# A graph network on one core: the recurrent layer's first state turned to features by VectorE squares and a DRAM trip

## The chip, the cores and the metric

The kernel runs on one core of a Trainium2 chip. The core has five engines with queues of their own: TensorE (PE, with its weight loads PEld) multiplies matrices into PSUM, VectorE (DVE) and ScalarE (ACT) work elementwise, GpSimd (POOL) does small things here, and SyncE (SP) issues DMAs. The metric is the device time of one execution in microseconds; lower is better. All arithmetic is in float32.

## The reference

A batch of 32 graphs with 512 nodes and 128 features per node passes four layers, each `x = x + layer(relu(layernorm(x)))`. All share one adjacency matrix. Cut to what is computed:

```python
# x: (32, 512, 128), adj: (512, 512)
# layer 0: graph convolution
x = x + einsum(A_norm, h) @ W.T + b            # A_norm: normalized adj + I
# layer 1: gated recurrent layer, five steps; h starts as relu(layernorm(x))
def step(h):
    m  = einsum('nm,bmd->bnd', adj, h)         # both of its matrices are adj
    av = concatenate([m, m], -1)
    u3 = h @ u3_w.T + u3_b
    z  = sigmoid(av @ w3_w.T + w3_b + u3)
    r  = sigmoid(av @ w4_w.T + w4_b + u3)
    hv = tanh(av @ w5_w.T + w5_b + (r * h @ u5_w.T + u5_b))
    return (1 - z) * h + z * hv
x = x + step(step(step(step(step(h)))))
# layers 2 and 3: graph attention (leaky relu, masked softmax over neighbours)
x = x + elu(softmax(mask(leaky(e_src + e_dst))) @ (h @ W))
x = x + softmax(mask(leaky(e_src + e_dst))) @ (h @ w)
```

The step needs its state `h` in two layouts. The product with `adj` sums over nodes, so it wants nodes on the partitions. The gates sum over features, so they want features on the partitions.

## The kernel before

The program is drawn up as a list of operations with an engine, a cost, a due time, and the tiles read and written. A greedy list scheduler simulates the engines with these costs and fixes, before the program is built, in which order each engine gets its instructions and which buffer each value uses. Every engine then runs its own list in order. Two batches make a pair; products with `adj` are done for a pair together with seven block products in place of eight.

The buffers that matter below (cut):

```python
    plan = Plan({
        "bank": tiles(8, TOKENS, "bank", psum),
        "lane": list(range(LANES)),
        "x": tiles(13, TOKENS, "x"),
        "h": tiles(LANES, [P, 2, 2 * D], "h"),
        "sq": tiles(2, [P, Q, W * C], "sq"),
        "far": tiles(4, [Q, W, Q, W * C], "far", dram),
        "hT": tiles(LANES + 2, TOKENS, "hT"),
# ... cut
}, 174, 0.08)
```

`h` is the state with nodes on the partitions, `hT` the state with features on them. `sq` and `far` serve trips through DRAM. `LANES = 6` bounds the batches that are in the recurrent layer at one time.

The recurrent layer's start, for each batch of a pair. `norm_relu` writes `h`; `to_features` makes `hT` from it with four TensorE transposes into a PSUM bank, and ScalarE copies the bank to SBUF:

```python
    def ggnn(pair, due):
        hs, hTs, lanes = [], [], []
        for b in pair:
            lane, h, hT = Val("lane"), Val("h", 2), Val("hT")
            op("SP", 0.0, due - 3, lambda: None, r=[xs[b]], w=[lane], delay=0)
            op("SP", 0.0, due - 3, lambda: None, r=[lane], w=[h], delay=0)
            norm_relu(b, h, due - 3)
            p = to_features(h, due - 2, hT)
            op("ACT", A, due - 2, lambda p=p, hT=hT: nc.scalar.copy(flat(hT.t), flat(p.t)), r=[p], w=[hT])
            hs.append(h)
            hTs.append(hT)
            lanes.append(lane)
        for s in range(STEPS):
            now = due + LANES * s
            ms = products(*hs, of_adj, now)
            for i, b in enumerate(pair):
                hs[i], hTs[i] = step(b, s, ms[i], hTs[i], now + i, lanes[i])
```

```python
    def to_features(y, due, *then):

        p = Val("bank")

        def turns():
            for c in range(C):
                nc.tensor.transpose(p.t[:, c, :], chunk(y, c), ident.t)
        op("PE", C * TURN, due, turns, r=[y, ident], w=[p, *then])
        return p
```

The step reads `hT` first in the second matmul of its gate (`reset`), after the products `m`. Its new state is in feature layout; the way back to `h` for the next product is `shuttle`:

```python
    def step(b, s, m, hT, due, lane):
        gate, r, rh, z = Val("bank"), Val("r"), Val("rh"), Val("z")

        def reset():
            nc.tensor.matmul(flat(gate.t), gates.t[:, 0, :], flat(m.t), start=True, stop=False)
            nc.tensor.matmul(flat(gate.t), gates.t[:, 1, :], flat(hT.t), start=False, stop=True)
        op("PE", 2 * MM, due + 0.2, reset, r=[m, hT, gates], w=[gate])
        op("ACT", A, due, lambda: nc.scalar.activation(flat(r.t), flat(gate.t), AF.Tanh, bias=gate_b["w4"].t, scale=0.5),
           r=[gate, gate_b["w4"]], w=[r])
        op("DVE", V, due - 5, lambda: nc.vector.scalar_tensor_tensor(flat(rh.t), flat(r.t), 1.0, flat(hT.t), op0=ALU.add, op1=ALU.mult),
           r=[r, hT], w=[rh])
        op("PE", MM, due + 0.3, lambda: nc.tensor.matmul(flat(gate.t), gates.t[:, 2, :], flat(m.t), start=False, stop=True,
                                                   skip_group_check=True), r=[m, gates], w=[gate])
# ... cut: update gate, candidate, and the new state "new"
        if not last:
            shuttle(new, None, h, True, due, due - 5)
            return h, new
```

`shuttle` is the trip that the kernel already has. VectorE transposes 32x32 blocks into `sq`; four DMAs write it to DRAM, and two (or one) read it back so that the blocks land on the partitions where they belong:

```python
    def shuttle(src, squares, dst, halves, due, soon):


        sq, far = Val("sq"), Val("far", Q)
        if halves:
            for a in range(2):
                op("DVE", 0.34, soon, lambda a=a: nc.vector.transpose(
                    sq.t.rearrange("p q (a j l) -> p a q l j", a=2, l=2)[:, a],
                    flat(src.t).rearrange("p (a l q i) -> p a q l i", a=2, l=2, q=Q)[:, a]), r=[src], w=[sq])
        else:
            op("DVE", 0.61, soon, lambda: nc.vector.transpose(
                sq.t.rearrange("p q (c j) -> p q c j", c=C), flat(src.t).rearrange(squares, c=C, q=Q)), r=[src], w=[sq])
        for k in range(Q):
            op("SP", 0.44, due, lambda k=k: nc.sync.dma_start(
                far.t[:, :, k, :].rearrange("q i f -> i q f"), sq.t[k * W:(k + 1) * W]), r=[sq], w=[far[k]], delay=4)
        if halves:
            for a in range(2):
                op("SP", 0.4, due, lambda a=a: nc.sync.dma_start(
                    dst.t[:, a, :].rearrange("p (k f) -> p k f", k=Q),
                    far.t.rearrange("q i k (a f) -> a (q i) k f", a=2)[a]), r=[far], w=[dst[a]], delay=5)
        else:
            op("SP", 0.4, due, lambda: nc.sync.dma_start(
                dst.t if dst.kind != "h" else dst.t.rearrange("p a (k f) -> p (a k) f", k=2), far.t.rearrange("q i k f -> (q i) k f")),
               r=[far], w=[dst], delay=5)
```

It runs after all steps but the fifth, for the fifth step's result, and for the input of the attention layers; the last pairs take TensorE transposes instead, because then nothing is left to hide a trip behind.

Of the kernel before, what the change touches and what calls it, by code (L numbers as in the profile page):

```python
# [18 lines left out]
W = 32  # L19
Q = P // W  # L20
NEAR = 4
EASE = 0
LANES = 6


# [17 lines left out]
class Plan:  # L43
# [8 lines left out]
    def op(self, engine, cost, due, emit, r=(), w=(), delay=None):  # L52
        o = Op(engine, cost, due, emit, self.DELAY[engine] if delay is None else delay)
        o.id = len(self.ops)
        before = {}
        for items, writes in ((r, False), (w, True)):
            for item in items:
                v, parts = item if isinstance(item, tuple) else (item, None)
                parts = range(len(v.writers)) if parts is None else [parts]
                if v not in o.vals:  # L60
                    o.vals.append(v)
                    v.uses += 1
                for c in parts:
                    before.update((p.id, p) for p in v.writers[c])
                    if writes:
                        before.update((p.id, p) for p in v.readers[c])
        for items, writes in ((r, False), (w, True)):
            for item in items:
                v, parts = item if isinstance(item, tuple) else (item, None)
                for c in range(len(v.writers)) if parts is None else [parts]:  # L70
                    if writes:
                        v.writers[c], v.readers[c] = [o], []
                    else:
                        v.readers[c].append(o)
        before.pop(o.id, None)
        for p in before.values():
            p.then.append(o)
        o.waits = len(before)
        self.ops.append(o)
# [72 lines left out]
def gnn_stack(ctx: ExitStack, tc: tile.TileContext, a: dict, out: bass.AP):  # L152
    nc = tc.nc
    x, adj = a["x"], a["adj"]
    B, N, D = x.shape
    C = N // P
# [9 lines left out]
    def flat(t):  # L166
        return t.rearrange("p c k -> p (c k)")
# [3 lines left out]
# [5 lines that stand above are left out]
# [26 lines left out]
    op = plan.op  # L202
    MM, MM1, TURN = 0.858, 0.224, 0.111
    V, A = 0.61, 0.585
# [27 lines left out]
    for c in range(C):  # L232
        e, q = (("SP", nc.sync), ("ACT", nc.scalar))[c % 2]
        op(e, 0.45, -1001, lambda c=c, q=q: q.dma_start(adj_sb.t[:, c, :], adj[c * P:(c + 1) * P, :]),
           w=[adj_sb[c]], delay=3.6)
    xs = []
    for b in range(B):
        v = Val("x", C)
        op("SP", 0.95, max(-995 + b, STEPS * b - 20) if b >= 8 else -995 + b, lambda v=v, b=b: nc.sync.dma_start(v.t, x[b].rearrange("(c p) d -> p c d", p=P)),
           w=[v], delay=3)  # L240
# [23 lines left out]
    for c in range(C):  # L264
        p = Val("bank")

        def turn_adj(c=c, p=p):
# [5 lines left out]
           r=[adj_sb[c]], w=[deg[c]])  # L273
# [17 lines left out]
    for m in range(C):  # L291
        op("DVE", 0.7, -797, lambda m=m: nc.vector.scalar_tensor_tensor(
            anT.t[:, m, :], adjT.t[:, m, :], dinv.t[:, m:m + 1], flat(drow.t), op0=ALU.mult, op1=ALU.mult),
           r=[adjT, dinv, drow], w=[anT[m]])
        op("DVE", 0.26, -797, lambda m=m: nc.vector.scalar_tensor_tensor(
            block(anT.t, m), ident.t, dinv2.t[:, m:m + 1], block(anT.t, m), op0=ALU.mult, op1=ALU.add),
           r=[ident, dinv2], w=[anT[m]])
# [19 lines left out]
    for l in (2, 3):  # L317
        far = Val(None, C)
# [12 lines left out]
        for c in range(C):  # L331
            op("SP", 0.4, 4 + l, lambda l=l, c=c, far=far: nc.sync.dma_start(
                maskT[l].t[c * W:(c + 1) * W], far.t[:, :, c, :].rearrange("q i n -> i q n")),
               r=[far], w=[maskT[l][c]], delay=2.2)
# [33 lines left out]
    for k, u, half in (("w4", "u3", True), ("w3", "u3", True), ("w5", "u5", False)):  # L368
        gate_b[k] = fixed([P, 1], "gate_b" + k)
        op("DVE", 0.1, -14, lambda k=k, u=u: nc.vector.tensor_add(gate_b[k].t, raw["b" + k].t, raw["b" + u].t),  # L370
           r=[raw["b" + k], raw["b" + u]], w=[gate_b[k]])
# [4 lines left out]
    for i, l in enumerate((2, 3)):  # L376
        p = Val("bank")
        op("PE", 0.3, -9, lambda i=i, l=l, p=p: nc.tensor.matmul(p.t[:, 0, :2], gats.t[:, i, :], a_pair[l].t, start=True, stop=True),
           r=[gats, a_pair[l]], w=[p])
# [46 lines left out]
# [11 lines that stand above are left out]
# [19 lines left out]
        else:  # L456
            op("SP", 0.4, due, lambda: nc.sync.dma_start(
                dst.t if dst.kind != "h" else dst.t.rearrange("p a (k f) -> p (a k) f", k=2), far.t.rearrange("q i k f -> (q i) k f")),
               r=[far], w=[dst], delay=5)

    def products(h1, h2, factors, due):

        x1, x2, S = (h1[0], h1[1]), (h2[0], h2[1]), Val("S", 4)
        HV, HM, HA = 0.34, 2 * 0.432, 0.26

        def part(item):
            v, a = item
            return v.t[:, a, :]  # L470

        def combine(o, u, v, f):
            op("DVE", HV, due - 5, lambda: f(part(o), part(u), part(v)), r=[u, v], w=[o])  # L473
        add, sub = nc.vector.tensor_add, nc.vector.tensor_sub
        combine(S[2], x1[0], x2[0], sub)
        combine(S[0], x2[0], x2[1], add)
        combine(S[1], S[0], x1[0], sub)
        combine(S[3], x1[1], S[1], sub)
        m1, m2, p1, u2, u4, r, t = Val("m", 2), Val("m", 2), Val("half"), Val("half"), Val("half"), Val("bank"), Val("bank")

        def times(r, item, k, fresh, *also):
            def two():
                u = part(item).rearrange("p (f l) -> p l f", l=2)
                for l in range(2):
                    nc.tensor.matmul(low(r), u[:, l, :], factors[k][0]()[:, l, :], start=fresh and l == 0, stop=l == 1,  # L485
                                     skip_group_check=not fresh)
            op("PE", HM, due, two, r=[item, factors[k][1]], w=[r, *also])

        def copy(o, r, out):
            op("ACT", HA, due, lambda: nc.scalar.copy(out(), low(r)), r=[r], w=[o])  # L490

        def low(v):
            return flat(v.t)[:, :2 * P]

        def high(v):
            return flat(v.t)[:, 2 * P:]
        def add_up(o, u, out):
            op("DVE", HV, due - 5, lambda: nc.vector.tensor_add(out(), u.t, low(t)), r=[u, t], w=[o])  # L498

        times(r, x1[0], 0, True, m1, m2, t, p1, u2, u4)  # L500
        copy(p1, r, lambda: p1.t)
        times(t, x1[1], 3, True)
        add_up(m1[0], p1, lambda: low(m1))
        times(r, S[1], 1, False)
        copy(u2, r, lambda: u2.t)
        times(t, S[2], 4, True)
        times(r, S[0], 2, False)
        copy(u4, r, lambda: u4.t)
        add_up(m2[1], u4, lambda: high(m2))
        times(t, x2[1], 6, False)  # L510
        add_up(m2[0], u2, lambda: low(m2))
        times(r, S[3], 5, False)
        copy(m1[1], r, lambda: high(m1))
        return m1, m2
# [32 lines left out]
    def ggnn(pair, due):  # L547
        hs, hTs, lanes = [], [], []
        for b in pair:
            lane, h, hT = Val("lane"), Val("h", 2), Val("hT")  # L550
            op("SP", 0.0, due - 3, lambda: None, r=[xs[b]], w=[lane], delay=0)
            op("SP", 0.0, due - 3, lambda: None, r=[lane], w=[h], delay=0)
            norm_relu(b, h, due - 3)
            p = to_features(h, due - 2, hT)
            op("ACT", A, due - 2, lambda p=p, hT=hT: nc.scalar.copy(flat(hT.t), flat(p.t)), r=[p], w=[hT])
            hs.append(h)
            hTs.append(hT)
            lanes.append(lane)
# [7 lines that stand above are left out]
# [29 lines left out]
        h = None if last else Val("h", 2)  # L595
        if due >= STEPS * B - EASE:
            p = to_features(new, due + 2, *([] if last else [h]))
# [164 lines left out]
```

## Time and profile before

The kernel takes 1664.14 us (median of three runs, 1663.68 to 1665.16). The profiled execution has a span of 1661.8 us.

| engine | busy us | share of the span | instructions |
|---|---|---|---|
| TensorE matmuls (PE) | 1634.7 | 98% | 7422 |
| TensorE weight loads (PEld) | 1176.3 | 71% | 7422 |
| VectorE (DVE) | 1362.7 | 82% | 3836 |
| ScalarE (ACT) | 734.8 | 44% | 1657 |
| GpSimd (POOL) | 143.2 | 9% | 136 |
| DMA, mean of 16 engines | | 34% | 311,423 packets |

How to read it: busy time is the time in which at least one instruction of the engine ran. TensorE's instructions overlap, so their listed durations add up to more than its busy time. A float32 matmul appears as two instructions, a transpose as one. In the chain of waits the profiler goes back from the last instruction, each time to what released it, and so names the engines that set the end. "A <- B" in the list of waits says that A's engine stood idle before A until B was done. "SPq" is SyncE's queue, which issues the DMAs.

The TensorE transposes of the first state are those that write `bank` from `ident` and `h` (128 instructions, for 32 batches); ScalarE's copies of them write `hT` from `bank` (32).

### The profile page before, as it was taken

Reading aid. Unit: us, or ns where it says so; the run is one execution under the profiler, and the core shown is the slowest. Engines: PE = TensorE matmul, PEld = TensorE weight load, DVE = VectorE, ACT = ScalarE, POOL = GpSimd, SP = SyncE. Lnnn points to the kernel's source line nnn. Section 1 sums busy time; section 2 is a strip of 40 time slices with the busy share of each in tenths; the row PEclk is TensorE's granted clock in tenths of the full one; section 3 lists DMA queues with packets and bytes.
Section 4 is the critical chain, followed back from the end, with each engine's and each line's share of the span. In section 5 each row is a group of like instructions: output and inputs, shape, how many; then the busy total and the mean of one; then the engine's idle time right before and its main releaser. Section 6 shows DMA issues by size and latency. Waiting matters only on the chain.

```text
span 1661.8 us, 23750 instructions
## 1 busy us (share of the span) xinstructions
PE 1634.7 (98%) x7422; PEld 1176.3 (71%) x7422; DVE 1362.7 (82%) x3836; ACT 734.8 (44%) x1657; POOL 143.2 (9%) x136
## 2 busy tenths in 40 slices
PE   7999999999999999999999999999999999999998
PEld 5766667677776777777677776777777777766677
DVE  8966778888878888888788888888888878777888
ACT  4643453535345354433534335353443534333433
POOL 2200000001001110000100000000000000000100
PEclk9999999999999999999999999999999999999999
DMA  5222333433334343342423334333242423434100
GB/s 153 51 70 58 83 83 95 115 80 99 90 89 108 84 105 87 91 113 73 122 71 99 98 92 108 90 96 95 77 121 64 108 70 91 106 90 114 27 26 27
DMA packets 311423, 146.17 MB, mean 88 GB/s; under 512 B 150400, under 2 KB 292864, under 8 KB 311296
## 3 DMA queue, kind: packets, MB, share of 16 engines
q1 hardware_dynamic: 311008, 144.12, 34.4%
q8 instruction: 59, 0.97, 0.2%
q14 instruction: 68, 0.56, 0.1%
q10 hardware_dynamic: 288, 0.52, 0.1%
HBM read 80.48 MB, written 64.08 MB: 87 GB/s over the span
## 4 chain that ended last, share of the span: by engine, by line
PE 92%; DVE 5%; ACT 1%; issue 1%; DMA 0%; POOL 0%; SPq 0%; DVEq 0%; POOLq 0%; ACTq 0%
PE bank L485 33%; PE bank L699 12%; PE bank L570 8%; PE bank L569 8%; PE bank L576 8%; PE bank L583 8%; PE bank L584 8%; PE bank L644 3%; PE bank L541 2%; PE bank L688 1%; PE bank L432 1%; DVE st L390 1%; PE bank L520 0%; ACT y L407 0%; POOL rstd L397 0%
## 5 line engine op out<-in xcount | busy, mean ns | idle before, releaser
L485 PE MATMUL bank<-made,S 128*128 128x256 f32 x1140 | 276.3, 380 | 3.9 <-DVE S L473 1.8
L397 POOL TENSOR_TENSOR rstd<-ve,mhalf 128x4 f32<-128x4 f32 x128 | 141.4, 1107 | 1491.0 <-DVE ve L395 1193.6
L485 PEld LDWEIGHTS bank<-made,S 128*128 128x128 f32 x1140 | 218.1, 196 | 45.5 <-issue 19.0
L490 ACT COPY half<-bank 128x256 f32<-128x256 f32 x285 | 105.3, 370 | 256.9 <-PE bank L485 254.9
L699 PEld LDWEIGHTS bank<-h_gat,e 128*128 128x128 f32 x1792 | 208.1, 192 | 12.7 <-issue 10.8
L572 ACT ACTIVATE r<-bank,gate_bw 128x512 f32<-128x512 f32 x160 | 109.6, 686 | 230.0 <-PE bank L570 218.7
L699 PE MATMUL bank<-h_gat,e 128*128 128x129 f32 x1792 | 208.5, 275 | 0.0
L574 DVE SCALAR_TENSOR_TENSOR rh<-r,hT 128x512 f32<-128x512 f32 x160 | 109.8, 687 | 100.6 <-ACT r L572 99.9
L679 DVE SCALAR_TENSOR_TENSOR e<-row,h_gat,maskT 128x512 f32<-128x512 f32 x256 | 181.3, 742 | 2.8 <-ACT row L666 2.8
L588 DVE TENSOR_TENSOR hv<-hv,hT 128x512 f32<-128x512 f32 x160 | 109.4, 683 | 67.6 <-ACT hv L586 67.2
L576 PE MATMUL bank<-m,wT 128*128 128x512 f32 x320 | 163.7, 593 | 0.0
L583 PE MATMUL bank<-m,wT 128*128 128x512 f32 x320 | 163.6, 593 | 0.0
L569 PE MATMUL bank<-m,wT 128*128 128x512 f32 x320 | 163.4, 592 | 0.0
L570 PE MATMUL bank<-hT,wT 128*128 128x512 f32 x320 | 163.4, 592 | 0.0
L584 PE MATMUL bank<-rh,wT 128*128 128x512 f32 x320 | 163.4, 592 | 0.0
L586 ACT ACTIVATE hv<-bank,gate_bw 128x512 f32<-128x512 f32 x160 | 109.5, 684 | 118.7 <-PE bank L584 117.5
L485 PE MATMUL bank<-adjT,h 128*128 128x256 f32 x640 | 157.8, 380 | 1.5 <-ACT h L407 1.5
L498 DVE TENSOR_TENSOR m<-half,bank 128x256 f32<-128x256 f32 x285 | 117.6, 413 | 43.2 <-ACT half L490 22.8
L485 PEld LDWEIGHTS bank<-adjT,h 128*128 128x128 f32 x640 | 121.7, 196 | 25.9 <-issue 12.1
L578 ACT ACTIVATE z<-bank,gate_bw 128x512 f32<-128x512 f32 x160 | 109.5, 684 | 49.5 <-PE bank L576 48.2
L390 DVE BATCH_NORM_STATS2 st<-x 128x6 f32<-128x128 f32 x512 | 121.6, 278 | 0.4
L570 PEld LDWEIGHTS bank<-hT,wT 128*128 128x128 f32 x320 | 60.8, 190 | 76.5 <-issue 76.5
(116 smaller groups left out, 2247.6 us busy)
## 6 DMA issues: line engine op xcount, KB each, us to landing
far<-sq SPq DMA_DIRECT2D x832, 64.0 KB
h<-far SPq DMA_DIRECT2D x248, 128.0 KB
gT<-far SPq DMA_DIRECT2D x56, 256.0 KB
row<-line SPq DMA_DIRECT2D x56, 256.0 KB
x<-in_x_dram SPq DMA_DIRECT2D x32, 256.0 KB
out_dram<-x SPq DMA_DIRECT2D x32, 256.0 KB
h<-far SPq DMA_DIRECT2D x28, 256.0 KB
far_mask<-mask SPq DMA_DIRECT2D x8, 128.0 KB
```

The source lines that it names most:

```text
L390: op("DVE", 0.21, due, lambda c=c: nc.vector.bn_stats(st.t[:, c, :], xb.t[:, c, :]), r=[xb[c]], w=[st[c]])
L397: op("POOL", 1.0, due, lambda: nc.gpsimd.tensor_tensor(rstd.t, ve.t, mhalf.t, ALU.pow), r=[ve, mhalf], w=[rstd])
L485: nc.tensor.matmul(low(r), u[:, l, :], factors[k][0]()[:, l, :], start=fresh and l == 0, stop=l == 1, skip_group_check=not fresh)
L498: op("DVE", HV, due - 5, lambda: nc.vector.tensor_add(out(), u.t, low(t)), r=[u, t], w=[o])
L569: nc.tensor.matmul(flat(gate.t), gates.t[:, 0, :], flat(m.t), start=True, stop=False)
L570: nc.tensor.matmul(flat(gate.t), gates.t[:, 1, :], flat(hT.t), start=False, stop=True)
L574: op("DVE", V, due - 5, lambda: nc.vector.scalar_tensor_tensor(flat(rh.t), flat(r.t), 1.0, flat(hT.t), op0=ALU.add, op1=ALU.mult), r=[r, h ...
L576: op("PE", MM, due + 0.3, lambda: nc.tensor.matmul(flat(gate.t), gates.t[:, 2, :], flat(m.t), start=False, stop=True, skip_group_check=Tru ...
L583: nc.tensor.matmul(flat(cand.t), gates.t[:, 3, :], flat(m.t), start=True, stop=False)
L584: nc.tensor.matmul(flat(cand.t), u5T.t[:, 0, :], flat(rh.t), start=False, stop=True)
L679: op("DVE", 0.68, due + 3, lambda j=j: nc.vector.scalar_tensor_tensor(e.t[:, j, :], row.t, h.t[:, j, D + 1:D + 2], maskT[l].t[:, j, :], op ...
L699: nc.tensor.matmul(pt()[:, c, :D + 1], e.t[:, j, i * P:(i + 1) * P], h.t[:, j, :D + 1], start=(j == 0), stop=(j == C - 1))
```

## The change

For batches 2 to 27, all but the first two and the last four, the first state's feature layout is no longer made by TensorE and ScalarE. VectorE makes squares of `h` (two instructions), four DMAs write the squares to DRAM, and four DMAs read them back into `hT`, each for 32 of the 128 nodes of every chunk. The buffers `sq` and `far` are those of the existing trips. `hT` gets four parts, so that each read is tracked alone. The aim is to take the transposes from TensorE. The due times of the squares and of the DMAs are 1 and 0.5 earlier than that of the transposes was, since the trip is longer.

```diff
--- before.py
+++ after.py
@@ -20,6 +20,7 @@
 Q = P // W
 NEAR = 4
 EASE = 0
+FAR0, FAR1 = 2, 4
 LANES = 6
 
 
@@ -458,6 +459,21 @@
                 dst.t if dst.kind != "h" else dst.t.rearrange("p a (k f) -> p (a k) f", k=2), far.t.rearrange("q i k f -> (q i) k f")),
                r=[far], w=[dst], delay=5)
 
+    def shuttle_first(h, hT, due, soon):
+
+        sq, far = Val("sq"), Val("far", Q)
+        for a in range(2):
+            op("DVE", 0.34, soon, lambda a=a: nc.vector.transpose(
+                sq.t.rearrange("p k (a l i) -> p a k l i", a=2, l=2)[:, a],
+                h.t.rearrange("p a (k j l) -> p a k l j", k=Q, l=2)[:, a]), r=[h[a]], w=[sq])
+        for q in range(Q):
+            op("SP", 0.44, due, lambda q=q: nc.sync.dma_start(
+                far.t[:, :, q, :].rearrange("k j f -> j k f"), sq.t[q * W:(q + 1) * W]), r=[sq], w=[far[q]], delay=4)
+        for q in range(Q):
+            op("SP", 0.4, due, lambda q=q: nc.sync.dma_start(
+                hT.t.rearrange("p c (q i) -> q p c i", q=Q)[q], far.t.rearrange("k j q (c i) -> q (k j) c i", c=C)[q]),
+               r=[far[q]], w=[hT[q]], delay=5)
+
     def products(h1, h2, factors, due):
 
 
@@ -547,12 +563,15 @@
     def ggnn(pair, due):
         hs, hTs, lanes = [], [], []
         for b in pair:
-            lane, h, hT = Val("lane"), Val("h", 2), Val("hT")
+            lane, h, hT = Val("lane"), Val("h", 2), Val("hT", Q)
             op("SP", 0.0, due - 3, lambda: None, r=[xs[b]], w=[lane], delay=0)
             op("SP", 0.0, due - 3, lambda: None, r=[lane], w=[h], delay=0)
             norm_relu(b, h, due - 3)
-            p = to_features(h, due - 2, hT)
-            op("ACT", A, due - 2, lambda p=p, hT=hT: nc.scalar.copy(flat(hT.t), flat(p.t)), r=[p], w=[hT])
+            if FAR0 <= b < B - FAR1:
+                shuttle_first(h, hT, due - 2.5, due - 3)
+            else:
+                p = to_features(h, due - 2, hT)
+                op("ACT", A, due - 2, lambda p=p, hT=hT: nc.scalar.copy(flat(hT.t), flat(p.t)), r=[p], w=[hT])
             hs.append(h)
             hTs.append(hT)
             lanes.append(lane)
```

For `shuttle_first`, the write takes 32 partitions x 4 pieces of 512 bytes, and each read 128 partitions x 4 pieces of 128 bytes.

## The prediction

> **What bounds the kernel now.** I read the busy shares first, then the idle time of TensorE stretch by stretch, then the chain of waits, and last the single instructions that the change touches. The busy shares and the chain on the page of the kernel before:
>
> ```profile
> PE 1634.7 (98%) x7422; PEld 1176.3 (71%) x7422; DVE 1362.7 (82%) x3836; ACT 734.8 (44%) x1657; POOL 143.2 (9%) x136
> ...
> PE 92%; DVE 5%; ACT 1%; issue 1%; DMA 0%; POOL 0%; SPq 0%; DVEq 0%; POOLq 0%; ACTq 0%
> ```
>
> TensorE is busy in 98% of the span and makes 92% of the chain that ended last. Busy alone can mislead, so I looked at where the missing 27.1 us (1661.8 less 1634.7) lie. Stretches of the span; the columns are start:end, length, busy us (instructions) of PE, PEld, DVE, ACT, POOL, then clock, DMA share and GB/s:
>
> ```profile
> 0.00:30.00 30.00, 20.60 (x95) 14.22 (x95) 23.02 (x96) 13.35 (x31) 7.07 (x13) 1.00 0.62 176
> 30.00:60.00 30.00, 29.27 (x125) 22.36 (x126) 29.57 (x118) 20.03 (x49) 6.93 (x7) 1.00 0.33 92
> 60.00:100.00 40.00, 40.00 (x158) 28.57 (x157) 34.13 (x126) 21.87 (x48) 8.20 (x8) 1.00 0.20 48
> ...
> 700.00:800.00 100.00, 100.00 (x459) 72.94 (x458) 82.80 (x231) 43.09 (x100) 7.34 (x7) 1.00 0.37 94
> ...
> 1600.00:1662.00 62.00, 50.95 (x385) 45.15 (x383) 51.20 (x162) 22.28 (x63) 6.46 (x6) 0.96 0.08 22
> ```
>
> From 60 to 1500 us TensorE never rests for more than a few tenths of a microsecond, at full clock. The idle time lies in the first 30 us and after 1500 us. All 26 batches that the change touches (2 to 27) begin their recurrent layer inside the full stretch. So a microsecond taken off TensorE there is a microsecond off the end, provided nothing new makes TensorE wait; and work put on any other engine costs nothing until it does.
>
> [...] one 128x512 matmul is listed at 593 ns, yet pairs of them start 0.86 us apart, 0.43 us each. I therefore price the removed transposes by the distance between starts and not by their listed duration. [...] The new reads use 128-byte pieces, which no transfer type of comparable volume in the kernel before does; the mean here is 29.4 ns of one DMA engine per packet, worked out below, and no trace yet shows the 128-byte case.
>
> **The change part by part.**
>
> Removed from TensorE: four 128x128 transposes per batch, 26 batches, 104 instructions. The rows that give the costs, first the groups (line, engine, operation, output<-input, shapes, count, busy us and mean ns of one, idle before), then a piece of TensorE's timeline:
>
> ```profile
> L432 PE MATMUL bank<-ident,h 128*128 128x128 f32 x128 | 19.8, 283 | 0.6 <-ACT h L407 0.6
> L555 ACT COPY hT<-bank 128x512 f32<-128x512 f32 x32 | 18.1, 586 | 1.9 <-PE bank L432 1.3
> L442 DVE STREAM_TRANSPOSE sq<-hT 128x256 f32<-128x256 f32 x248 | 105.5, 433 | 1.4
> ```
>
> ```profile
> 704.28 0.59 PE L485 MATMUL bank<-made,S 128*128 128x256 f32 x2
> 704.71 1.11 PE L432 MATMUL bank<-ident,h 128*128 128x128 f32 x8
> 705.66 1.04 PE L485 MATMUL bank<-made,S 128*128 128x256 f32 x4
> ```
>
> The group's 283 ns would give 104 x 0.283 = 29 us, which is far too much[...]. Its busy time, 19.8 us for 128, or 155 ns each, still contains the overlap with the next matmul. The timeline has the true price: eight transposes start at 704.71 and the next work starts at 705.66, so 0.95 us for eight, 0.119 us each. The other places where four stand alone give 0.46 to 0.47 us. So 26 x 0.47 = 12.2 us leave TensorE. At the thirteen pairs concerned I added up the distances from the first transpose to the next work as they stand, with the four places where TensorE hesitated (0.73, 0.86, 0.63 and 0.87 us instead of 0.47): 13.4 us. The gain is between these two if nothing new waits.
>
> Removed from ScalarE: 26 copies x 0.586 = 15.2 us. ScalarE is 44% busy, so this gives nothing. One PSUM bank of eight is also free for the time of a transpose and its copy; nothing in the waits shows the banks as scarce, so I count nothing.
>
> Added to VectorE: 52 block transposes of 128x256. The existing ones of that size take 0.433 us, so 22.5 us, and VectorE goes from 1362.7 to 1385, or from 82% to 84% of a shorter span. The new ones read pairs two elements apart instead of writing so; I take the same duration. They are off the path as long as VectorE's queue delays nothing that TensorE waits for.
>
> Added to the DMA queue of SyncE: 104 writes at the existing 0.434 us of issue (median of the 832 like them) and 104 reads at 0.524 us (median of the 248 reads that also have 512 pieces): 45 + 54 = 99 us of issuing, 6% of the span. Packets: a write is 32 x 4 pieces of 512 bytes, 128; a read is 128 x 4 pieces of 128 bytes, 512; so 26 x 4 x (128 + 512) = 66,560 on top of 311,423. Now 34.4% of 16 engines' 1661.8 us over 311,008 packets is 29.4 ns per packet. At that price the addition is 66,560 x 29.4 ns / 16 = 122 us, 7% of the span, and the DMA share rises from 34% to about 42%. Not a bound.
>
> Moved: the state in feature layout arrives later after normalization. Before, two links (0.47 us of transposes, 0.59 of copy). After: 0.87 us of VectorE, 1.74 of write issues, a landing, 2.1 of read issues, a landing. In the timeline the writes issued from 706.13 to 708.69 were followed by their reads at 711.58, so a landing takes at most 2.9 us. Estimate of the trip from these: 0.9 + 1.7 + 2.9 + 2.1 + 2.9 = 10.5 us.
>
> What hides it: the first user is the second matmul of the gate, after the seven matmul groups of the pair's adjacency product. The instruction order of the changed program, built by a list scheduler that allows 4 and 5 us for the two landings, has the first product of pair (2, 3) 14 rows of TensorE ahead of the first gate that reads a state from the trip, and most rows are worth 0.86 us: 12 us, besides the time from normalization to product. In the order before it was 12 rows. So the order was drawn with the trip in view, and the trip fits.
>
> Sum on the path: -12.2 to -13.4 for TensorE, plus what returns as new waits. I put 1 to 3 us for these. 1664.1 - 12.8 + 2 = 1653 us, 0.7% less.
>
> **Rivals.**
>
> *The trip comes late and TensorE waits at the first gate.* SyncE issues in order, so a write that waits for a buffer holds everything behind it, the recurrence's own trips too. Total us, times and longest, of waits:
>
> ```profile
> SPq L449 <- DVE sq L442: 189.6, 70, 16.4
> ...
> SPq L449 <- DMA h<-far: 83.9, 42, 2.8
> ...
> SPq L453 <- DMA far<-sq: 21.8, 32, 2.4
> ```
>
> ```profile
> PEld bank L485 <- DMA h<-far: 0.3, 1, 0.3
> ```
>
> For it: the four DRAM buffers are already waited for 42 times, and the two square buffers now serve 234 trips instead of 208, 12.5% more. Against it: with 208 trips of the same kind TensorE lost 0.3 us to a landing in the whole run, and the SyncE queue mostly waits for VectorE to give it something. If each of the 13 pairs lost 1 us the time would be 1664 again; at 2 us each, 1677.
>
> *VectorE becomes the bound.* Between 30 and 60 us it is busy 29.57 of 30, and up to 86% per 100 us later. The first new squares (batches 2 and 3) fall near that start. A few microseconds may be lost there; in the middle 16% of VectorE stays free. If every added VectorE microsecond counted, the time would be 1664 - 13 + 22 = 1673; I don't believe it, since TensorE was full beside a VectorE at 86%.
>
> *The new order deals the end differently.* Every engine's order changes from the second pair on. After 1500 us TensorE idles about 15 us (3.3, 0.7 and 11.0 in three stretches), and the last four batches are dealt anew. That could give or take some 5 us for reasons that have nothing to do with the transposes.
>
> **Range and chances.** The middle is 1653. The best case is all 13.4 us and a lucky end, 1646. The bad side is longer: 5 us of stalls at the start and 5 at the end make 1662. I put 8 in 10 on 1646 to 1662. Faster by over 2% needs 33 us, more than twice all that leaves TensorE: 0.01. Slower by over 2% needs every pair to stall by over 3 us: 0.03. The rest, 0.96, is within 2%.
>
> **What the profile after would show.** If right: transposes of the normalized state down from 128 to 24; TensorE's busy time lower by about 12 to 16 us and still 98%; ScalarE's copy of the state at 6 instead of 32; VectorE near 1385 us; DMA packets near 378,000 and their share near 40%; no wait of TensorE on the landing of the state above 1 us in total. It would be wrong if TensorE's idle time grew by 10 us or more between 60 and 1500 us, with the landing, VectorE's gate operations or the adjacency combinations as releasers, if a new 128-byte read cost far more than 29 ns per packet, or if the idle time after 1500 us changed by more than 5 us.

## The result and the profile after

| | median us | runs | lowest to highest |
|---|---|---|---|
| before | 1664.13 | 6 | 1663.30 to 1665.16 |
| after | 1659.45 | 6 | 1659.22 to 1660.46 |

The ratio is 0.9973, 95% interval 0.9961 to 0.9986. The change gains 4.7 us, 0.3%. It is a gain, but under half of the 11 us forecast.

The busy shares and the chain on the page after:

```profile
PE 1624.3 (98%) x7318; PEld 1163.4 (70%) x7318; DVE 1375.8 (83%) x3888; ACT 722.5 (44%) x1631; POOL 141.0 (9%) x136
...
q1 hardware_dynamic: 380896, 157.77, 39.1%
...
PE 94%; DVE 3%; ACT 1%; DMA 0%; SPq 0%; issue 0%; POOL 0%; DVEq 0%; POOLq 0%; ACTq 0%
```

TensorE has 104 instructions fewer and is busy 10.4 us less (1634.7 to 1624.3). The span fell by only 4.4 us (1661.8 to 1657.4). So TensorE's idle time grew by 6.0 us, from 27.1 to 33.1. The share of 98% and the chain's 94% would not have told: the same stretches as before do. (Columns: start:end, length, busy us (instructions) of PE, PEld, DVE, ACT, POOL, clock, DMA share, GB/s.)

```profile
0.00:30.00 30.00, 21.26 (x94) 15.13 (x94) 22.74 (x94) 12.51 (x29) 7.06 (x13) 0.94 0.62 176
...
60.00:100.00 40.00, 40.00 (x155) 28.28 (x154) 36.57 (x137) 21.08 (x49) 8.86 (x8) 1.00 0.44 91
...
700.00:800.00 100.00, 100.00 (x468) 72.25 (x467) 85.93 (x242) 40.11 (x90) 7.40 (x7) 1.00 0.43 102
800.00:900.00 100.00, 96.03 (x432) 68.98 (x431) 82.79 (x246) 43.13 (x99) 9.82 (x9) 0.98 0.43 103
```

The 100 us from 700 are as full as they were before. The next 100 us lose 4 us of TensorE and some of its clock. Before, the same stretch read:

```profile
800.00:900.00 100.00, 99.77 (x452) 71.42 (x451) 84.96 (x243) 45.38 (x105) 8.98 (x9) 1.00 0.38 95
```

TensorE's list of waits after (what waited <- for whom: us in total, times, longest) has one long new entry:

```profile
PE bank L501 <- ACT half L506: 8.8, 11, 4.0
PE bank L270 <- DMA e<-in_adj_dram: 4.8, 1, 4.8
PE bank L707 <- DVE e L698: 4.3, 4, 1.8
```

L501 is the adjacency product, and `half` is ScalarE's copy of a partial sum of that product in a PSUM bank. The next group adds to the same bank, so it must wait for the copy. Before, this wait was 4.0 us in 8 times with 1.3 as the longest; the 4.0 us now is one single event. The timeline of TensorE around it (start, us, engine, line, operation, count, in brackets the idle time before it and its releaser):

```profile
800.18 1.89 PE L501 MATMUL bank<-made,S 128*128 128x256 f32 x8
801.91 1.03 PE L501 MATMUL bank<-adjT,h 128*128 128x256 f32 x4
806.90 1.62 PE L501 MATMUL bank<-adjT,S 128*128 128x256 f32 x4 [3.97 <-ACT half L506]
808.32 1.91 PE L501 MATMUL bank<-made,h 128*128 128x256 f32 x4
810.02 1.43 PE L501 MATMUL bank<-anT,pair 128*128 128x256 f32 x4
811.29 1.02 PE L588 MATMUL bank<-m,wT 128*128 128x512 f32 x2
```

And ScalarE in the same time:

```profile
801.20 0.51 ACT L408 ACTIVATE h<-x,off,rstd 128x128 f32<-128x128 f32 x1 [0.44 <-DVE x L630]
802.26 1.65 ACT L408 ACTIVATE y<-x,off,rstd 128x128 f32<-128x128 f32 x4 [0.55 <-DVE off L405]
803.81 0.87 ACT L408 ACTIVATE h<-x,off,rstd 128x128 f32<-128x128 f32 x2
804.58 1.63 ACT L408 ACTIVATE y<-x,off,rstd 128x128 f32<-128x128 f32 x4
806.12 0.48 ACT L408 ACTIVATE h<-x,off,rstd 128x128 f32<-128x128 f32 x1
806.50 0.35 ACT L506 COPY half<-bank 128x256 f32<-128x256 f32 x1
```

ScalarE runs twelve normalization activations in a row, over 5 us (with one wait of 0.55 us for VectorE), and only then the copy that TensorE needs, because its fixed list has them in that order. ScalarE is 44% busy over the span; in these 5 us it is the bound.

The event costs more than its idle time. Four products take 0.86 us, so the group at 806.90 should have started at 802.77: 4.13 us late. Then its first twelve instructions, to 811.29, take 4.39 us; at the usual distance of 0.216 us between starts they take 2.59. That is 1.80 us more, and the stretches tell why:

```profile
803.00:807.40 4.40, 0.50 (x2) 0.48 (x3) 3.67 (x17) 4.40 (x13) 2.01 (x2) 1.00 0.70 179
807.40:810.80 3.40, 3.40 (x9) 2.73 (x9) 1.49 (x6) 1.37 (x4) 0.00 (x0) 0.50 0.69 160
```

After the rest, TensorE was granted half its clock for 3.4 us. So this one event costs 4.13 + 1.80 = 5.9 us.

A balance of the whole run, from TensorE's first start to its last, made of the distances between starts: I priced each instruction by the usual distance to the next of its kind (0.429 us for 512 columns, 0.216 for 256, 0.112 for 128, 0.110 for a transpose) and called the rest of every distance excess, whether wait or slow clock.

| us | before | after | difference |
|---|---|---|---|
| work at usual distances | 1619.42 | 1607.98 | -11.44 |
| excess | 32.32 | 39.37 | +7.05 |
| of it between 800 and 900 us | 0.6 | 6.0 | +5.4 |

The sum, -4.4, is the difference of the spans. (The balance takes the 11.44 us from the prices; what it measures is the excess.) 60% of the gain was given back, three quarters of that in one place. The same prices show it on the way: the TensorE work still to come, the transposes of the first state not counted, is 831.3 us before and 826.6 after at 800 us, so the changed kernel is 4.7 us ahead. At 820 us it is 812.7 and 812.6, and the lead is gone.

### The profile page after: what moved, and what is told of

Read it like the earlier page. It is cut to its first block, busy times and chain, and to the rows that moved or that the text cites. A ratio compares the mean times of both kernels' runs of the same rounds, so it can differ in the third digit from the quotient of the medians.

```text
span 1657.4 us, 23932 instructions
## 1 busy us (share of the span) xinstructions
PE 1624.3 (98%) x7318; PEld 1163.4 (70%) x7318; DVE 1375.8 (83%) x3888; ACT 722.5 (44%) x1631; POOL 141.0 (9%) x136
## 2 busy tenths in 40 slices
DMA packets 381312, 159.81 MB, mean 96 GB/s; under 512 B 206976, under 2 KB 362752, under 8 KB 381184
## 3 DMA queue, kind: packets, MB, share of 16 engines
q1 hardware_dynamic: 380896, 157.77, 39.1%
## 4 chain that ended last, share of the span: by engine, by line
PE 94%; DVE 3%; ACT 1%; DMA 0%; SPq 0%; issue 0%; POOL 0%; DVEq 0%; POOLq 0%; ACTq 0%
PE bank L501 34%; PE bank L718 12%; PE bank L588 8%; PE bank L589 8%; PE bank L595 8%; PE bank L602 8%; PE bank L603 8%; PE bank L663 3%; PE bank L557 2%; PE bank L707 1%; DVE e L698 1%; PE bank L433 1%; PE bank L536 0%; PE bank L690 0%; SPq L450 0%
## 5 line engine op out<-in xcount | busy, mean ns | idle before, releaser
L501 PE MATMUL bank<-made,S 128*128 128x256 f32 x1140 | 274.4, 380 | 3.5 <-DVE S L489 2.1
L501 PEld LDWEIGHTS bank<-made,S 128*128 128x128 f32 x1140 | 219.3, 196 | 44.2 <-issue 18.5
L718 PEld LDWEIGHTS bank<-h_gat,e 128*128 128x128 f32 x1792 | 208.8, 192 | 17.0 <-issue 15.2
L501 PE MATMUL bank<-adjT,h 128*128 128x256 f32 x640 | 161.1, 382 | 1.5 <-ACT h L408 1.5
L501 PEld LDWEIGHTS bank<-adjT,h 128*128 128x128 f32 x640 | 122.5, 197 | 27.5 <-issue 12.7
```

The costliest lines, as they stand in the source:

```text
L718: nc.tensor.matmul(pt()[:, c, :D + 1], e.t[:, j, i * P:(i + 1) * P], h.t[:, j, :D + 1], start=(j == 0), stop=(j == C - 1))
```

## The experiments

Medians in us; the ratio is to the kernel before in runs on the same chip (its median 1664.16 beside the first four, 1663.89 beside the next four, 1664.49 beside the last). The last three columns are TensorE's idle time in the profiled execution, worked out as length less busy time: in the first 60 us, from 60 to 1490, and after 1490.

| run | median | ratio, 95% interval | idle to 60 | 60 to 1490 | after 1490 |
|---|---|---|---|---|---|
| before | 1664.13 | 1 | 10.1 | 2.1 | 14.9 |
| after | 1659.45 | 0.9973, 0.9961 to 0.9986 | 9.6 | 7.3 | 16.2 |
| e1_left_out | 1661.68 | 0.9986, 0.9979 to 0.9993 | 10.7 | 7.7 | 14.3 |
| e2_copies_moved | 1656.27 | 0.9950, 0.9935 to 0.9965 | 9.7 | 4.6 | 16.1 |
| e3_no_squares | 1660.60 | 0.9975, 0.9966 to 0.9983 | 10.2 | 7.3 | 16.1 |
| e4_one_read | 1659.73 | 0.9973, 0.9962 to 0.9983 | 10.2 | 7.4 | 16.1 |
| e5_half_earlier | 1653.29 | 0.9935, 0.9920 to 0.9950 | 9.6 | 4.2 | 11.3 |
| e6_from_batch_8 | 1670.58 | 1.0038, 1.0024 to 1.0052 | 9.4 | 9.5 | 18.5 |
| e7_before_redrawn | 1670.11 | 1.0039, 1.0024 to 1.0054 | 9.9 | 4.3 | 18.4 |
| e8_copies_due_earlier | 1653.28 | 0.9939, 0.9924 to 0.9953 | 10.1 | 1.5 | 15.9 |
| e9_before_best_draw | 1661.68 | 0.9983, 0.9975 to 0.9991 | 10.4 | 0.9 | 12.8 |
| e10_after_best_draw | 1649.81 | 0.9915, 0.9900 to 0.9930 | 10.2 | 4.2 | 11.7 |
| e11_copy_out_too | 1662.09 | 0.9985, 0.9979 to 0.9992 | 9.9 | 6.5 | 14.7 |
| e12_before_copies_earlier | 1669.84 | 1.0034, 1.0021 to 1.0047 | 9.8 | 1.4 | 20.1 |

My theory after the result: the transposes are worth what was forecast, and the newly drawn order, in which ScalarE comes late with one product's copies, takes more than half of it back. Rivals: the transposes are worth less than they look, since TensorE would have waited anyway; VectorE's added work, or the added packets, take it back.

### The transposes left out, nothing put in their place

Before's own order; the 104 transposes of batches 2 to 27 are not executed. ScalarE's copy reads the unnormalized `x` instead, so that it costs the same (ScalarE is busy 734.5 us against 734.8).

```diff
-    def to_features(y, due, *then):
+    def to_features(y, due, *then, leave=False):
...
         def turns():
+            if leave:
+                return
...
+            leave = 2 <= b < B - 4
-            p = to_features(h, due - 2, hT)
-            op("ACT", A, due - 2, lambda p=p, hT=hT: nc.scalar.copy(flat(hT.t), flat(p.t)), r=[p], w=[hT])
+            p = to_features(h, due - 2, hT, leave=leave)
+            op("ACT", A, due - 2, lambda p=p, hT=hT, b=b, leave=leave: nc.scalar.copy(
+                flat(hT.t), flat(xs[b].t if leave else p.t)), r=[p], w=[hT])
```

> The kernel before, in its own order, with the 104 TensorE transposes of batches 2 to 27 left out (ScalarE copies the un-normalized input into hT instead, so the values differ) and no trip put in their place. It asks what the transposes alone are worth when nothing is drawn anew. If their price is what TensorE's start distances say (104 x 0.110 us), the time falls by 11 to 12 us, to about 1652.5. If TensorE is not really the bound in the middle, it falls by clearly less, under 8.

Measured: 1661.68, only 2.5 us below before. The idle time from 60 to 1490 us grew from 2.1 to 7.7 us, and by the balance the excess of the whole run grew by 8.4 us, which leaves 3.0 of the 11.4. It is not one event here; the wait for `half` grew from 4.0 us in 8 times to

```profile
PE bank L487 <- ACT half L492: 8.8, 14, 1.3
```

What happened is seen where a pair begins. TensorE before:

```profile
805.50 1.90 PE L485 MATMUL bank<-adjT,h 128*128 128x256 f32 x8
807.23 1.03 PE L485 MATMUL bank<-made,S 128*128 128x256 f32 x4
808.10 0.63 PE L432 MATMUL bank<-ident,h 128*128 128x128 f32 x4
808.96 1.14 PE L485 MATMUL bank<-adjT,S 128*128 128x256 f32 x4 [0.23 <-ACT half L490]
```

The same place without the transposes:

```profile
803.63 1.89 PE L487 MATMUL bank<-adjT,h 128*128 128x256 f32 x8
805.39 1.14 PE L487 MATMUL bank<-made,S 128*128 128x256 f32 x4
807.60 1.14 PE L487 MATMUL bank<-adjT,S 128*128 128x256 f32 x4 [1.07 <-ACT half L492]
```

In before's order the second batch's transposes stood where TensorE had to wait for ScalarE's copy anyway. Without them the wait behind them comes to light: 1.07 us in place of 0.23. So with a fixed order the transposes are worth little: the first rival holds there, and more strongly than it had put it. It does not yet say what they are worth in an order drawn without them.

### ScalarE's own copy left out as well

On top of the experiment before, the copy to `hT` is not made either; a DMA loads `x` into `hT`.

```diff
-            op("ACT", A, due - 2, lambda p=p, hT=hT, b=b, leave=leave: nc.scalar.copy(
-                flat(hT.t), flat(xs[b].t if leave else p.t)), r=[p], w=[hT])
+            op("ACT", A, due - 2, lambda p=p, hT=hT, b=b, leave=leave: nc.sync.dma_start(
+                hT.t, x[b].rearrange("(c p) d -> p c d", p=P)) if leave else nc.scalar.copy(flat(hT.t), flat(p.t)), r=[p], w=[hT])
```

> As the run with the transposes left out of the kernel before's own order (1661.7), but ScalarE's copies of batches 2 to 27 are left out as well; a plain load of the input fills hT instead, with other values. If the waits that appeared there came from ScalarE, which still made the copy between the products' copies at each pair's start, they shrink and the time falls to 1653 to 1657. If they came from the normalizations and the products' own copies, it stays at 1660 to 1663.

Measured: 1662.09, the same as with the copy. ScalarE did 13 us less (721.6 busy against 734.5), and the wait for `half` is still 6.7 us in 12 times. ScalarE's copies of the state were not what held TensorE at the pair starts; what stays on ScalarE there are the normalizations and the product's copies.

### The late copies of one product moved ahead

After, with six instructions of the one product at 800 us put further up in their engines' lists: two copies on ScalarE, two additions on VectorE, two groups on TensorE. All work is done.

```diff
+        for i, before in ((4047, 3224), (4048, 3621), (4051, 3225), (4049, 4928), (4050, 3623), (4052, 4908)):
+            o = self.ops[i]
+            order.remove(o)
+            order.insert(order.index(self.ops[before]), o)
```

> The changed kernel with six instructions of one adjacency product (two ScalarE copies, two VectorE additions, two TensorE groups) moved ahead, at the one place near 803 us where TensorE stood for 4 us behind twelve normalizations on ScalarE. Theory 'queue order': the normalizations in front of the copy are the cause; the stall and the halved clock after it vanish and the time falls by 4 to 6 us, to about 1654. Theory 'no other work': TensorE has nothing else in its order there that could run, so the wait moves to the next gate operations of the same pair and the time stays within 1.5 us of 1659.4.

Measured: 1656.27 (1654.19 to 1657.28), 3.2 us below after, whose runs it does not overlap. The stretch of the event, in after:

```profile
800.00:820.00 20.00, 16.03 (x48) 9.84 (x47) 13.61 (x56) 11.20 (x25) 4.31 (x4) 0.91 0.60 144
```

and with the six moved:

```profile
800.00:820.00 20.00, 18.73 (x70) 12.28 (x70) 17.21 (x64) 12.75 (x32) 4.31 (x4) 1.00 0.72 164
```

TensorE rests 1.27 us instead of 3.97 and keeps its full clock. The stall itself is gone: the group that started at 806.90 us starts at 802.83, without a rest. In its place stands a new rest of 1.07 us at 809 us, in the gates of the same pair, until ScalarE's `r` is done; so theory 'no other work' holds for a quarter of the wait. The edit takes away 2.7 us of rest and 1.8 of lost clock. The span of the profiled execution fell by less, 3.0 us, because TensorE ran at half clock for 3.4 us from 1633.6 us, which it did not do there in after (mean clock from 1500 to 1640 us 0.99 against 1.00): by the balance 4.1 us come back between 800 and 900 us, and 1.2 are lost after 1600. The stall is thus a cause of the missing gain, and ScalarE's order is the cause of the stall.

### VectorE's added work left out

After's order; the 52 block transposes are not executed, so the DMAs carry what was in the buffers.

```diff
-            op("DVE", 0.34, soon, lambda a=a: nc.vector.transpose(
-                sq.t.rearrange("p k (a l i) -> p a k l i", a=2, l=2)[:, a],
-                h.t.rearrange("p a (k j l) -> p a k l j", k=Q, l=2)[:, a]), r=[h[a]], w=[sq])
+            op("DVE", 0.34, soon, lambda: None, r=[h[a]], w=[sq])
```

> The changed kernel in its own order with the 52 block transposes on VectorE left out (the DMAs carry stale data). Theory 'VectorE': the 22.5 us that it gained push back the others, so that several us return: 1652 to 1656. Theory 'drawn order': VectorE's load is hidden, within 1 us of 1659.4, and the 4 us stall near 803 us stays.

Measured: 1660.60, no faster than after. VectorE is busy 15.3 us less (1375.8 to 1360.5), and the stall stands as it was: `PE bank L499 <- ACT half L504` has again 8.9 us in 11 times, 4.0 the longest. VectorE is not what took the gain.

### The four 128-byte reads made one

After's order; one DMA that reads whole rows of 2,048 bytes in place of the four. It moves the same bytes, but to other places of `hT` than the gates expect.

```diff
             op("SP", 0.4, due, lambda q=q: nc.sync.dma_start(
-                hT.t.rearrange("p c (q i) -> q p c i", q=Q)[q], far.t.rearrange("k j q (c i) -> q (k j) c i", c=C)[q]),
+                flat(hT.t), far.t.rearrange("k j q f -> (k j) (q f)")) if q == Q - 1 else None,
```

> The changed kernel in its own order with the four reads in 128-byte pieces replaced by a single read in whole rows, issued where the fourth stood (the values land in the wrong places). Theory 'trip': small packets and four issues delay this trip and those behind it; the time falls by several us. Theory 'drawn order': nothing waits for these reads, so within 1 us of 1659.4, while the DMA packets fall by some 50,000.

Measured: 1659.73 against 1659.45, though there are 51,167 packets fewer (381,312 to 330,145). The trip is hidden, and so are its small pieces. In the list of TensorE's waits after, no entry names `hT` as the thing landed; three of its weight loads waited for a write to a trip's buffer (`far`), 0.2 us each.

### One due time half a unit earlier

After, with one number changed. The work of every engine is the same; the scheduler draws another order.

```diff
-                shuttle_first(h, hT, due - 2.5, due - 3)
+                shuttle_first(h, hT, due - 2.5, due - 3.5)
```

> The changed kernel with one number changed: the squares are due half a unit earlier (3.5 instead of 3). The work is the same to the instruction; only the list scheduler's order differs, and in it no TensorE group stands behind the twelve normalizations. Theory 'drawn order': the stall is gone, TensorE's work is unchanged, and the time is 1650 to 1652. Theories 'VectorE' and 'trip': the same load and the same trips, so 1658 to 1661.

Measured: 1653.29, 6.2 us below after, which is the forecast of the change itself. TensorE from 800 to 820 us is busy for all of 20.00 us, and the longest wait for `half` is

```profile
PE bank L501 <- ACT half L506: 4.7, 10, 0.5
```

The idle time fell by 8.0 us against after: 3.1 in the middle and 4.9 at the end (TensorE's busy time rose by 2.4 us; its clock was lower at the end, 0.96 from 1500 to 1640). The balance, which counts idle time and slow clock together, shows which of the two places made the gain: the excess fell by 5.4 us in all and by 5.9 between 800 and 900 us, so the rest of the run gave nothing. The stall is no property of the change. It belongs to the one order that the scheduler drew.

### Before, redrawn

The control: the kernel before, with the transposes due half a unit earlier. The same work again.

```diff
-            p = to_features(h, due - 2, hT)
-            op("ACT", A, due - 2, lambda p=p, hT=hT: nc.scalar.copy(flat(hT.t), flat(p.t)), r=[p], w=[hT])
+            p = to_features(h, due - 2.5, hT)
+            op("ACT", A, due - 2.5, lambda p=p, hT=hT: nc.scalar.copy(flat(hT.t), flat(p.t)), r=[p], w=[hT])
```

> The kernel before, with no trip, and the transposes and copies of the first state due half a unit earlier (2.5 instead of 2). The work is the same to the instruction. Theory 'drawn order': a mere redraw moves the time by as much as the change did; this order has a small gap in nearly every pair, so 1667 to 1671. The other theories have nothing that would move it: 1663 to 1665.

Measured: 1670.11, 6.2 us above before. Of it 3.5 us are idle time at the end and 2.2 in the middle. A mere redraw moves the kernel by as much as the change does. One redraw doesn't rank before's order; but a second one further below is over 5 us slower too, and the best of 225 only 2.8 us faster, so before seems to have had a good order for its work.

### The change for twenty batches instead of 26

```diff
-FAR0, FAR1 = 2, 4
+FAR0, FAR1 = 8, 4
```

> The changed kernel with the trip for batches 8 to 27 only: 20 batches in place of 26. By the count of transposes alone it should be 20 x 0.44 = 8.8 us faster than before (1655.3), and theories 'VectorE' and 'trip' would make it at most as slow as the change, 1655 to 1660. Theory 'drawn order': in its order the pattern of the stall stands in two places, so two waits of about 4 us, each followed by a halved clock, and 1663 to 1667, no faster than before, though less was changed.

Measured: 1670.58, slower than before although 80 transposes are gone, and 3.6 us above the range that I had expected. Two stretches show the same event as after's, with the clock lowered each time:

```profile
400.00:420.00 20.00, 16.03 (x55) 11.49 (x54) 14.45 (x64) 9.77 (x24) 4.31 (x4) 0.83 0.56 132
1200.00:1220.00 20.00, 16.03 (x76) 12.94 (x75) 15.78 (x67) 10.22 (x27) 4.31 (x4) 0.91 0.56 130
```

I had counted the two stalls and not the end, where the idle time is 2.3 us above after's; and after the first stall the clock was halved for 6.8 us, twice as long as in after. A count of batches is not a dose here: each setting is a new draw.

### ScalarE's product copies due earlier, with and without the change

After and before, each with the copies of the adjacency products due 5 units earlier, so that the scheduler puts them ahead of the normalizations. The edit is the same in both:

```diff
-            op("ACT", HA, due, lambda: nc.scalar.copy(out(), low(r)), r=[r], w=[o])
+            op("ACT", HA, due - 5, lambda: nc.scalar.copy(out(), low(r)), r=[r], w=[o])
```

> The changed kernel with ScalarE's copies of the adjacency products due five units earlier, as VectorE's additions of the same products already are. The scheduler then puts them ahead of normalizations everywhere, and the order is drawn anew. Theory 'drawn order': no stall of over 1 us in the middle, 1651 to 1654. Other theories: 1658 to 1661.

> The kernel before with the same shift that gave 1653.3 in the changed kernel: ScalarE's copies of the products due five units earlier. It makes a pair at equal settings. Theory 'drawn order': its order has no large gap in the middle but another end, 1666 to 1670, so the pair's difference is 13 to 17 us, more than the transposes take; without such luck of the draw the pair would differ by 11 us.

Measured: with the change 1653.28; without it 1669.84. In both the middle is nearly free of idle time (1.5 and 1.4 us), so the rule does what it was made for. Before gets slower all the same, because its end is dealt badly: 20.1 us of idle time after 1490, against 14.9, and 17.1 us at half clock there, against 3.4 (the last microseconds, in which TensorE is done, not counted; the mean clock from 1490 to 1664 us is 0.95 against 0.98). At this setting the change gains 16.6 us. At the first it gained 4.7.

### A good order for each

From here I let the scheduler draw many orders of each kernel, varied only in due times and in one weight of the scheduler, and took for each the one that ended first in the scheduler's own account.

```diff
 # before, best draw
-            op("ACT", HA, due, ...)
+            op("ACT", HA, due - 2, ...)
-            p = to_features(h, due - 2, hT)                 # and its copy
+            p = to_features(h, due - 1.5, hT)
 # after, best draw
-    }, 174, 0.08)
+    }, 174, 0.082)
-                shuttle_first(h, hT, due - 2.5, due - 3)
+                shuttle_first(h, hT, due - 2.5, due - 3.5)
```

> The kernel before, still without a trip, with the best of 225 orders that the list scheduler drew from it when due times were shifted (copies of the products due 2 earlier, first transposes due 1.5 before the step instead of 2). Same work as before. It asks how much of the change's gain is to be had from the order alone. Theory 'drawn order': 1658 to 1661. If the order of the kernel before was already as good as any: 1663 to 1665.

> The changed kernel with the best of as many orders (squares due 3.5 before the step instead of 3, and the scheduler's hurry factor 0.082 instead of 0.08). Same work as the change. Theory 'drawn order': 1649 to 1653, and the distance to the best order without the trip is again what the transposes take, 8 to 11 us. If the trip itself costs something, the distance is clearly smaller, under 6 us.

Measured: before's best 1661.68, after's best 1649.81. The first is 2.8 us below before, the second 9.6 us below after and 14.7 below before: the fastest version of this study (ratio 0.9915, 0.9900 to 0.9930). From 60 to 1490 us:

```profile
60.00:1490.00 1430.00, 1425.75 (x6232) 1010.56 (x6231) 1193.05 (x3314) 628.27 (x1397) 115.74 (x106) 1.00 0.42 101
```

VectorE carries 83% and the DMA engines 42% of this stretch, and TensorE rests 4.25 of 1430 us. Between the medians of the two good draws lie 11.9 us, between their profiled executions 10.0 (before's best was profiled in the fastest of its 15 runs): TensorE's busy time differs by 12.0 us (1633.7 and 1621.7), its idle time by 2.0 the other way. In this pair the 104 transposes are worth 10 to 12 us; it is one pair, and other good draws could lie elsewhere. Nor is each microsecond of a good draw the order's own. After's best draw rests as long in the middle as the order with the squares due half a unit earlier (4.2 us in both); it is 3.5 us faster, and in the profiled executions its TensorE ran at half clock for 3.4 us against 13.7 (mean clock over the span 0.999 against 0.996).

## Why the prediction was right and where it failed

**Removed from TensorE (12.2 to 13.4 us): nearly right.** Counted at 0.110 us each, the distance inside a row of transposes, 104 make 11.4 us; TensorE's busy time fell by 10.4 where I had put 12 to 16. I had read 0.119 us from a group of eight between matmuls, and 0.46 to 0.47 from groups of four; both distances contain the step to other work. The two good draws differ by 11.9 us in the median and by 10.0 in the profile.

**Removed from ScalarE (15.2 us): right in kind.** The copies to `hT` fell from 32 to 6 and ScalarE's busy time by 12.3 us, which gives nothing by itself, as the two left-out experiments on before show.

**Added to VectorE: right, and not a bound.** The 52 new instructions (groups of instructions, after: line, engine, operation, shapes, count, busy us and mean ns, idle before) took the predicted time:

```profile
L466 DVE STREAM_TRANSPOSE sq<-h 128x256 f32<-128x256 f32 x52 | 21.9, 431 | 0.1
```

VectorE's busy time rose by 13.1 us to 1375.8, not to 1385; the listed durations overlap with their neighbours, as TensorE's do: they add up to 1628.2 us, 23.5 more than before, in 1375.8 us of busy time. Without the new work it is no faster, so that rival falls.

**The trip: right.** It was hidden as the order promised. The packets rose by 69,889 (I had 66,560, 5% fewer; I had left out 16 packets of 4 bytes that each of the 208 added DMAs has in the trace), their share to 39.1% instead of 42%. The queue's time rose from 0.344 x 1661.8 to 0.391 x 1657.4 us of 16 engines, 76 us, or 17.5 ns for each added packet instead of the mean of 29.4. The new size is cheap by the packet and dear by the byte: in the trace after, a packet of 128 bytes takes 12.8 ns on average (54,144 packets) and one of 512 bytes 31.6, so a byte costs 1.6 times as much in the small one. With 51,167 of them taken out again the time does not move. The rival of a late landing falls.

**"A microsecond taken off TensorE there is a microsecond off the end, provided nothing new makes TensorE wait" and "I put 1 to 3 us for these": here it failed.** The term for new waits measured 7.0 us, and 5.4 of it lie between 800 and 900 us. I had looked for new waits at the landing, at VectorE and at the end. It came from ScalarE, which I had dismissed as 44% busy, and in the middle, where before showed TensorE full. Four runs tell what it is. Six instructions moved in that one place bring back 3.2 us. One due time moved by half a unit brings back 6.2 us with the same work. VectorE's work and the packets taken out bring back nothing. And the first half of the sentence doesn't hold either: in before's own order, with nothing new on any engine, 104 transposes less brought 2.5 us off the end, because some of them stood where TensorE would have waited for ScalarE. None of the signs of being wrong that I had named came: the idle time from 60 to 1490 us grew by 5.2 us and not by 10, that after 1490 by 1.3 and not by 5, and ScalarE's copy was not among the releasers in my list.

**The third rival, "the new order deals the end differently", had the right mechanism and the wrong place.** I knew that every engine's order changes from the second pair on, gave it 5 us, and tied it to the last four batches. In after the end lost only 1.3 us of idle time more. But the whole list is dealt anew, and a bad hand can lie anywhere: at 800 us in after, at 406 and 1209 in the variant for twenty batches, at the end in before redrawn. I should also have asked how good a hand before held: a redraw of the same work was 6.2 us worse. A full TensorE between 60 and 1500 us was a property of that order, not of the work.

**What stays open.** Why the scheduler puts the normalizations ahead of those copies in one draw and not in another was not traced. With the six instructions moved TensorE still rests 1.07 us for ScalarE's `r`, and I did not look for an edit that removes this too. Of the 7.0 us of new excess, 1.6 lie outside 800 to 900 us, in small pieces that were not traced. Nothing shows that the order of the last variant is the best there is.

## What to carry to other kernels

Where a scheduler fixes the order, a small change is two changes: the work that it saves, and a new draw of everything. Before a gain of half a per cent is believed or given up, redraw the kernel before and the kernel after several times with the same work, and compare good draw with good draw. And taking work off the full engine within a fixed order may bring little: look at what the next instruction behind that work would have waited for, for the removed work may only have covered a wait for an engine that is mostly idle.

## What the hardware showed

A stall of TensorE cost more than its idle time. A rest of 3.97 us occurs five times in the traces: in after, without the squares, with the one read, and twice with twenty batches. Each time the granted clock then fell to 0.50, for 3.41 us in two of the five and for 6.83 us in three. The mean clock shows it: over the 20 us around the rest it is 0.91 in after and at 1200 us with twenty batches, but 0.83 without the squares and at 400 us with twenty batches; over the 100 us from 800 it is 0.97 with the one read and without the squares, 0.98 in after. The 100 us around have 6.0 us of excess in after, where the halved clock lasted 3.41 us, and 7.3 without the squares, where the order is the same and it lasted 6.83. Why it lasted twice as long there was not shown.

A shorter rest went both ways. With ScalarE's own copy left out as well, a rest of 1.62 us at 1515 us, with none over 0.1 us in the 13 us before it, was followed by 3.41 us at half clock (mean clock from 1490 to 1664 us 0.97, against 0.98 in before); the same rest in before, at 1518 us, was not: the clock stayed at 1.00 from 1518 to 1535 us. So the waits of 4 us in this kernel cost 6.0 and 7.3 us where they were added up, and what a shorter one costs can't be read from its length.
